# A four-layer graph network on one core: the last step of its layer normalisation on two other engines, the graph's self-loops selected later, and all jobs in a new order

## The chip, the core and the metric

The kernel runs on one core of a Trainium2 chip. A core has five engines that run their own instruction streams in order and meet through semaphores: TensorE (matrix products, into PSUM), VectorE, ScalarE, GpSimd (called POOL in the profile, without access to PSUM) and SyncE, which issues most DMAs here. The metric is the device time of one execution in microseconds (us); smaller is better. A measurement is given as the median of several runs.

## What is computed

Inputs are x, 32 batches of 512 nodes with 64 features, and one 512 x 512 adjacency matrix with weights. Four layers follow one another, each on a normalised and rectified copy of x and each with a residual addition. Everything is float32. Cut to what matters:

```python
def _layernorm(x, axis=-1, eps=1e-5):
    m = jnp.mean(x, axis=axis, keepdims=True)
    v = jnp.var(x, axis=axis, keepdims=True)
    return (x - m) / jnp.sqrt(v + eps)

h = jnp.maximum(_layernorm(x), 0.0); x = x + L0(h, adj)   # 3 steps: v = W2 relu(W1 [v, adj v] + b1) + b2; node 0 is replaced first
h = jnp.maximum(_layernorm(x), 0.0); x = x + L1(h, adj)   # 2 layers: z = relu((adj z) W)
h = jnp.maximum(_layernorm(x), 0.0); x = x + L2(h, adj)   # 8 attention heads and one output head, scores h hT masked by adj
h = jnp.maximum(_layernorm(x), 0.0); x = x + L3(h, adj)   # attention with leaky-ReLU scores, adj with ones on its diagonal
```

## The kernel before

**Pairs.** The 32 batches are worked in 16 pairs. Nodes lie on the 128 partitions, so one pair's x is a tile of 128 x 512 (four blocks of nodes, two batches, 64 features).

**Jobs.** The program is cut into named jobs. A job `p.name` belongs to pair p. Each issues a few instructions on one or more engines, and the order in which the jobs are called is the program order of every engine's stream. Three strings give that order: HEAD and TAIL list jobs of given pairs, and ROUND lists `name:lag`, which is repeated for every pair with the pair's number shifted by the lag. Jobs that HEAD or TAIL names are left out of the rounds. No engine passes an instruction that waits, so a job's place decides both what it waits behind and what waits behind it.

**Names that matter here.**
- `F0` to `F32` (function `front`): layers 0 and 1 of a pair, in 33 steps. F0 to F2 are the first normalisation: F0 the mean (VectorE) with centring and squares (GpSimd, L423 and L425); F1 the sum of squares (VectorE, L428) and the power -1/2 (GpSimd, L432); F2 the last step z (L435), then node 0's row (L541, VectorE) and b2 added to x (L542, GpSimd). F3 and F4 transpose z. F5 to F16 are the three steps of layer 0, F17 and F18 the residual x1, which also loads the x of the pair after next. F19 to F21 normalise x1, F22 to F29 are layer 1 (L485 is the aggregation over the graph), F30 to F32 normalise x2.
- `zT`, `zE`: features transposed; `k`, `Y`: keys of two heads (L1139, L1150).
- For a unit of two heads (letters a to d and g to j) or of the output attention (f) and the last layer (e): `s` scores on TensorE (L641, L644), `r` masked product with the row maximum on VectorE (L650), `m` the maximum negated on GpSimd (L663), `x` exponentials on ScalarE (L670), `nA`, `nB` reciprocal on VectorE and scaling on GpSimd (L682), `t` 32 x 32 transposes on VectorE (L688), `v` the weighted sums on TensorE (L697, L925, and L1022 for the last pair). Scores have four PSUM buffers, which `r` frees.
- `us`, `w`, `y`, `o`, `c`: eviction, the head's weights (L738), leaky ReLU (L750), output projection (L758), joining.
- `oA`, `oB`, `oC`: the normalisation ahead of the last layer; `oA0`, `oA1` and so on for the last pair, whose two batches go separately.
- `loops0` to `loops3` (L376): four selections each on GpSimd, which put ones on the diagonal of A3, the third copy of the graph in SBUF; only jobs `r…e` read A3. `factor0` to `factor3` (L371) prepare the second copy, A2, `masks` the mask; `graph0` to `graph3` transpose the first copy.
- `ZQ`, `hQ`, `lQ`, `LQ`, `OQ`: DMAs that spread values over partitions.

**Loads.** SyncE issues, in order, x of pair 0, the graph's first copy, small weights, x of pair 1, A2 in two halves and A3 in two halves.

Of the kernel before, what the change touches and what calls it, by code (L numbers as in the profile page):

```python
# [21 lines left out]
def gnn_stack_kernel(  # L22
# [40 lines left out]
        0.weights 0.F0 0.joined 0.F1 0.F2 0.F3 0.F4 0.biases 0.F5 0.F6 0.graph2 0.graph3 0.graph1 0.graph0 1.F0 0.F7  # L63
        0.F8 0.bjoined 0.F9 0.loops1 0.loops0 0.F10 0.F11 0.masks 0.loops3 0.F12 1.F1 0.factor1 0.F13 0.F14
        0.factor2 0.F15 0.F16 0.F17 1.F2 0.factor3 0.F18 0.grams 0.F19 0.F20 1.F3 2.F0 0.F21 0.F22 0.F23 0.F24 0.F25
        0.F26 1.F4 0.F27 1.F5 0.factor0 0.F28 0.F29 1.F6 0.F30 1.F7 0.F31 1.F8 0.vectors 0.F32 2.F1 0.zT 0.zE 0.k0
        0.Y0 1.F9 0.s0a 1.F10 0.s1a 0.r1a 0.ZQ11 0.r0a 0.r2a 0.m0a 0.x0a 0.s3a 0.r3a 0.s2a 0.m1a 0.r7a 0.r6a 0.r4a
        0.ZQ13 0.x1a 0.s1b 0.m3a 0.r5a 0.s0b 0.k1 0.x3a 0.m2a 0.x2a 0.nAa 0.r3b 0.r2b 0.r1b 0.r0b 0.m1b 0.Y1 0.s3b
        0.nBa 0.t0a 0.r6b 0.s2b 0.r4b 0.r7b 0.x1b 0.m0b 0.ZQ01 0.t1a 0.x0b 0.ZQ03 0.r5b 0.s0c 0.s1c 0.m2b 0.m3b
        0.t2a 1.F11 0.x2b 0.nAb 0.r1c 0.r2c 0.x3b 0.r0c 0.r3c 0.nBb 0.t3a 1.F12 0.t0b 0.m1c 0.t1b 0.m0c 0.x1c 0.s3c  # L70
        1.F13 0.ZQ02 1.F14 0.t3b 0.ZQ00 0.ZQ10 0.x0c 0.t2b 0.r7c 0.r6c 0.s2c 0.vA0 0.vB0 0.r4c 2.F2 0.r5c 0.m3c
        0.s0d 0.m2c 0.vC0 0.vD0 0.r1d 0.nAc 0.r0d 0.s1d 0.m0d 0.x3c 0.t0c 0.x2c 0.us0 0.s2d 0.t1c 0.w00 0.x0d 0.w10
        0.nBc 0.r3d 0.y00 0.r2d 0.t2c 0.m1d 0.t3c 0.ZQ12 0.r5d 0.s3d 0.r7d 0.k2 0.loops2 0.r6d 0.y10 0.o0 0.x1d
        0.r4d 0.m3d 0.Y2 0.x3d 0.m2d 0.nAd 0.c0 0.x2d 0.s1g 1.F15 1.F16 0.r2g 0.s0g 0.t0d 0.nBd 0.t1d 0.r3g 0.t2d
        1.F17 0.t3d 0.s3g 1.F18 0.r7g 0.vA1 0.r6g 0.vB1 1.F19 0.r0g 0.r1g 0.m1g 0.vC1 3.F0 1.F20 0.m3g 0.x1g 0.vD1
        0.m0g 0.s0h 0.s1h 0.r0h 0.r1h 0.us1 0.w01 0.s2g 0.x0g 0.r3h 0.r2h 0.x3g 0.s2h 0.y01 0.k3 0.nAg 0.m0h 0.r4g
        0.r5g 1.F21 0.r4h 0.r5h 0.Y3 0.m2g 0.t0g 0.x2g 0.s3h 0.w11 0.r6h 0.m2h 0.m1h 0.s2i 0.y11 0.nBg 0.x1h 0.x2h
        0.t1g 1.F22 0.r4i 0.s0i 0.t2g 1.F23 1.F24 0.r7h 0.m3h 0.r5i 0.x3h 0.x0h 3.F1 0.s1i 0.r0i 0.nBh 1.F25 0.r1i
        0.o1 0.r3i 0.t3g 0.r2i 0.nAh 1.F26 0.t2h 0.t3h 0.m0i 1.F27 0.t0h 0.t1h 0.s3i 1.F28 0.s1j 0.c1 1.F29 0.m1i
        1.F30 0.x1i 0.vA2 0.r6i 0.m2i 0.vB2 0.x2i 0.x0i 0.vC2 0.r7i 0.vD2 0.s2j 0.r2j 0.m3i 1.F31 0.x3i 0.nAi 0.r3j  # L80
        0.us2 1.F32 1.zT 0.m1j 2.F3 0.nBi 0.s0j 1.zE 0.r5j 0.r4j 2.F4 0.w12 0.t0i 0.x1j 2.F5 0.t2i 0.s3j 1.ZQ00 2.F6
        0.r1j 0.r7j 1.k0 0.y12 0.r0j 0.r6j 0.w02 0.m2j 0.m0j 1.Y0 0.x2j 1.s0a 1.s1a 2.F7 0.t1i 1.r1a 0.m3j 0.t3i
        0.x0j 0.x3j 0.y02 0.nAj 1.r3a 1.r0a 0.D0 1.r2a 2.F8 1.ZQ01 0.t0j 1.m1a 0.o2 1.k1 1.s3a 0.nBj 1.x1a 0.f0
        1.s2a 0.t1j 0.t2j 1.Y1 0.c2 1.m0a 0.t3j 0.vA3 0.vB3 1.ZQ02 1.r4a 1.x0a 1.r5a 1.nAa 0.vC3 0.vD3 1.m2a 1.r7a
        0.us3 1.t1a 1.x2a 3.F2 1.r6a 1.m3a 1.t0a 1.s1b 1.s0b 1.r2b 1.x3a 1.r3b 1.m1b 1.x1b 2.F9 1.ZQ10 1.r1b 1.ZQ12
        1.r0b 1.m0b 2.F10 1.x0b 1.s3b 1.ZQ11 1.s2b 1.nBa 1.r7b 1.r4b 1.r6b 1.m3b 0.w13 1.r5b 1.t2a 0.y13 0.w03 1.x3b
# [24 lines left out]
        t2c:0 r2d:0 oN:2 s0d:0 w00:0 r3d:0 oV:2 r1d:0 s2d:0 r0d:0 s3d:0 m1d:0 r4d:0 x1d:0 m0d:0 w10:0 r5d:0 y00:0
        x0d:0 r7d:0 m2d:0 oD:2 oF:2 r6d:0 s1f:1 m3d:0 x2d:0 x3d:0 nAd:0 F15:-1 de:2 r3f:1 t3c:0 t0d:0 nBd:0 r2f:1
        y10:0 k2:0 t1d:0 t2d:0 F16:-1 t3d:0 o0:0 Y2:0 s6e:2 ZQ10:0 F17:-1 hQ1:1 c0:0 F18:-1 s0e:2 vA1:0 r0e:2 F19:-1
        s3e:2 s7e:2 r7e:2 s1e:2 vB1:0 r3e:2 s2e:2 r6e:2 lQ2:2 s0f:1 r2e:2 m3e:2 r1e:2 m1e:2 s5e:2 m0e:2 s4e:2 x0e:2
        m1f:1 F20:-1 r0f:1 x1e:2 hQ2:1 r5e:2 r1f:1 x3e:2 vC1:0 r4e:2 m2e:2 s3f:1 x2e:2 F21:-1 s2f:1 x1f:1 nAe:2
        vD1:0 m0f:1 us1:0 r7f:1 r6f:1 r4f:1 t0e:2 nBe:2 s0g:0 r5f:1 t1e:2 r1g:0 hQ3:1 m3f:1 s1g:0 x0f:1 w01:0 r2g:0
        r0g:0 w11:0 m2f:1 x3f:1 y01:0 nAf:1 x2f:1 m0g:0 r3g:0 t3e:2 t0f:1 y11:0 s3g:0 t2e:2 nBf:1 lQ1:2 x0g:0 lQ0:2
        s2g:0 r7g:0 r6g:0 F22:-1 m1g:0 F23:-1 o1:0 r4g:0 r5g:0 lQ3:2 t1f:1 m3g:0 s1h:0 m2g:0 t2f:1 c1:0 F24:-1 t3f:1
        x1g:0 F25:-1 ZQ12:0 s0h:0 x3g:0 nAg:0 r0h:0 r3h:0 r2h:0 x2g:0 vAE:1 r1h:0 m0h:0 m1h:0 vBE:1 vCE:1 x1h:0
        x0h:0 vDE:1 nBg:0 F0:-3 eu:1 t1g:0 t2g:0 s2h:0 t0g:0 s3h:0 nAh:0 t3g:0 r5h:0 r4h:0 t0h:0 r6h:0 k3:0 Y3:0  # L120
        r7h:0 m2h:0 et:1 s1i:0 s0i:0 m3h:0 ZQ13:0 x2h:0 er:1 F26:-1 x3h:0 r3i:0 r0i:0 nBh:0 r1i:0 t1h:0 t2h:0 r2i:0
        F27:-1 s3i:0 F28:-1 s2i:0 t3h:0 F29:-1 m0i:0 vA2:0 vB2:0 x0i:0 vC2:0 m1i:0 x1i:0 F30:-1 r4i:0 r7i:0 r6i:0
        F2:-2 m3i:0 F31:-1 nAi:0 r5i:0 m2i:0 vD2:0 x3i:0 s2j:0 F32:-1 t0i:0 us2:0 zT:-1 s1j:0 zE:-1 F3:-2 r5j:0 oA:1
        w12:0 x2i:0 F4:-2 r3j:0 r4j:0 r2j:0 y12:0 m2j:0 s0j:0 m1j:0 x1j:0 s3j:0 t1i:0 k0:-1 nBi:0 w02:0 r6j:0 r0j:0
        Y0:-1 r1j:0 r7j:0 t3i:0 s1a:-1 m3j:0 F5:-2 s0a:-1 r2a:-1 t2i:0 y02:0 m0j:0 r0a:-1 F6:-2 x0j:0 nAj:0 x3j:0
# [1220 lines left out]
```

## Time and profile before

| | |
|---|---|
| median of 3 runs | 2108.91 us |
| the three runs | 2110.44, 2103.96, 2108.91 us |
| the profiled execution | 2107.21 us |
| its span (first to last instruction) | 2105.4 us |
| mean granted clock of TensorE | 0.986 |
| A3's copies issued / landed | 29.2 and 29.8 / 42.5 us |
| first scores (L641) | 86.8 us |
| first weighted sums (L697) | 109.8 us |
| a repeat of the round | 123.08 us |
| the last twentieth (1998.8 to 2105.4): TensorE busy | 77.2 of 106.6 us |

The profile is that of one execution. Its first part gives each engine's busy time. Its second cuts the span into 40 slices of 52.6 us, and a digit is the busy share of a slice in tenths. A group of instructions has its line, engine, operation, output and inputs with shapes and count, then busy time and mean nanoseconds of one, then the engine's idle time ahead of it with what ended that. The chain of waits is followed back from the last instruction: at each step to whatever released it, or to the instruction before it on its engine. "issue" is time in which the profile shows nothing that was waited for. The ends of matrix products are modelled, so a busy TensorE is not always at its peak.

### The profile page before, as it was taken

The numbers are of one execution on the slowest core, as the hardware profiler recorded it, in microseconds if no ns is written. First come the engines' busy times: TensorE is split into PE (matmuls) and PEld (weight loads), VectorE is DVE, ScalarE is ACT, GpSimd is POOL, SyncE is SP. The second block draws the span as 40 slices with busy tenths as digits, with TensorE's granted clock in tenths as the row PEclk, the third lists the DMA queues.
The fourth block names the chain that finished last, engine by engine and source line by source line (L and its number), as shares of the span: only waits on it lengthen the run. The fifth ranks groups of instructions, "written<-read, shape, count | busy, mean of one in ns | idle before, by whom it ended". The sixth has DMA issues, their size and how long they took to land.

```text
span 2105.4 us, 91065 instructions
## 1 busy us (share of the span) xinstructions
PE 2023.7 (96%) x38941; PEld 1218.5 (58%) x38941; DVE 1842.8 (88%) x4205; ACT 1468.8 (70%) x3796; POOL 1274.8 (61%) x2161
## 2 busy tenths in 40 slices
PE   5799999999999999999999999999999999999985
PEld 3356566565556656555665655666565565655554
DVE  3588888989999999999999999999999998899955
ACT  1366667778686777867677786767778677677845
POOL 2356565766666576666657666665766656566543
PEclk9899999999999999999999999999999999999997
DMA  6101101112121111212111111111111111111213
GB/s 135 25 9 27 28 20 34 31 27 43 28 42 26 34 30 27 41 30 42 26 33 27 31 38 33 38 30 32 27 33 38 31 36 35 41 26 33 41 32 74
DMA packets 257626, 74.46 MB, mean 35 GB/s; under 512 B 240324, under 2 KB 249668, under 8 KB 257220
## 3 DMA queue, kind: packets, MB, share of 16 engines
q1 hardware_dynamic: 256768, 68.54, 15.6%
q8 instruction: 305, 5.00, 1.0%
q14 instruction: 101, 0.83, 0.1%
q10 hardware_dynamic: 452, 0.10, 0.0%
HBM read 16.52 MB, written 4.78 MB: 10 GB/s over the span
## 4 chain that ended last, share of the span: by engine, by line
PE 79%; DVE 11%; ACT 3%; POOL 2%; issue 2%; DMA 2%; SPq 0%; ACTq 0%; DVEq 0%; POOLq 0%
PE s L641 21%; PE mm L697 18%; PE mm L758 5%; PE mm L925 5%; PE mm L508 5%; PE s L644 5%; PE mm L738 5%; PE mm L485 4%; DVE sm L688 4%; DVE sm L650 4%; PE mm L1139 3%; PE mm L511 3%; ACT sm L670 2%; POOL sm L682 1%; PE mm L533 1%
## 5 line engine op out<-in xcount | busy, mean ns | idle before, releaser
L670 ACT ACTIVATE sm<-sm,nmx 128x512 f32<-128x512 f32 x1280 | 909.3, 716 | 221.7 <-POOL nmx L663 217.6
L682 POOL TENSOR_SCALAR sm<-sm,rs 128x512 f32<-128x512 f32 x1280 | 873.6, 704 | 275.7 <-DVE rs L680 263.9
L650 DVE CUSTOM_DVE_ANT_0 sm<-s,A 128x512 f32<-128x512 f32 x1264 | 808.1, 678 | 43.5 <-PE s L644 41.2
L688 DVE STREAM_TRANSPOSE sm<-sm 128x1024 f32<-128x1024 f32 x640 | 776.4, 1229 | 78.7 <-POOL sm L682 77.0
L641 PE MATMUL s<-ZZ,Y 64*64 64x512 f32 x4096 | 568.8, 600 | 5.9 <-DVE mx L650 5.7
L697 PE MATMUL mm<-sm,vq 32*64 32x256 f32 (+1 forms) x16640 | 492.9, 376 | 3.9 <-DVE sm L688 3.1
L697 PEld LDWEIGHTS mm<-sm,vq 32*64 32x64 f32 x16640 | 399.3, 132 | 106.9 <-issue 53.8
L663 POOL TENSOR_SCALAR nmx<-mx 128x2 f32<-128x2 f32 x640 | 141.4, 233 | 304.3 <-DVE mx L650 236.3
L641 PEld LDWEIGHTS s<-ZZ,Y 64*64 64x64 f32 x4096 | 143.1, 133 | 185.2 <-DVE mx L650 67.4
L644 PE MATMUL s<-NEGM,I2b 64*64 64x512 bf16 x2288 | 249.3, 376 | 0.0
L670 ACT ACTIVATION_READ_ACCUMULATOR sm<-sm,nmx 128x1 f32 x1280 | 246.3, 192 | 0.0
L644 PEld LDWEIGHTS <-I2b 64*64 64x64 bf16 x2288 | 81.2, 107 | 151.2 <-issue 148.9
L750 ACT ACTIVATE y<-mm,cols 128x512 f32<-128x512 f32 x256 | 161.1, 686 | 9.1 <-PE mm L738 7.6
L738 PE MATMUL mm<-us,Wh 64*64 64x512 f32 x1024 | 141.5, 590 | 1.3 <-ACT hT L478 0.8
L432 POOL TENSOR_TENSOR r<-ve,mhalf 128x8 f32<-128x8 f32 (+1 forms) x65 | 106.3, 1636 | 59.6 <-DVE ve L430 50.8
L423 POOL TENSOR_TENSOR xc<-x,nmu 128x512 f32<-128x512 f32 (+1 forms) x49 | 50.3, 1026 | 142.2 <-DVE nmu L421 135.6
L732 ACT COPY us<-mm 128x256 f32<-128x256 f32 x256 | 76.1, 380 | 85.1 <-PE mm L697 85.1
L485 PE MATMUL mm<-AT,z 128*128 128x512 f32 x256 | 121.4, 618 | 7.1 <-DVE z L435 6.3
L758 PE MATMUL mm<-y,Wo_sb 128*64 128x256 f32 x1024 | 124.1, 384 | 2.1 <-ACT y L750 2.1
L508 PE MATMUL mm<-AT,v 128*64 128x256 f32 x1024 | 117.6, 382 | 0.1
L925 PE MATMUL mm<-sm,vq 32*64 32x256 f32 x3712 | 111.4, 376 | 0.6 <-issue 0.6
L925 PEld LDWEIGHTS mm<-sm,vq 32*64 32x64 f32 x3712 | 101.1, 132 | 13.7 <-DVE rs L680 7.1
(151 smaller groups left out, 1875.6 us busy)
## 6 DMA issues: line engine op xcount, KB each, us to landing
vq<-z SPq DMA_DIRECT2D x512, 32.0 KB
HH<-cat SPq DMA_DIRECT2D x128, 64.0 KB
vq<-catT SPq DMA_DIRECT2D x240, 32.0 KB
vq<-h3n SPq DMA_DIRECT2D x240, 32.0 KB
A<-in_adj_dram SPq DMA_DIRECT2D x5, 1024.0 KB
xt<-in_x_dram SPq DMA_DIRECT2D x32, 128.0 KB
ZZ<-ZZ SPq DMA_DIRECT2D x32, 128.0 KB
out_dram<-xo SPq DMA_DIRECT2D x32, 128.0 KB
```

The costliest lines, as they stand in the source:

```text
L485: nc.tensor.matmul(pe, lhsT=v[:, m].rearrange("p j d -> p (j d)"), rhs=AT[:, m, :], start=(m == 0), stop=(m == NT - 1),)
L508: nc.tensor.matmul(ph[out_, :], lhsT=v[:, m, j, :], rhs=AT[:, m, h], start=False, stop=stop)
L641: nc.tensor.matmul(pss[half][R[ab], :], lhsT=lhsT, rhs=rhs, start=True, stop=False)
L644: nc.tensor.matmul(pss[half][R[ab], :], lhsT=I2b[R[half], :], rhs=NEGM[R[half], k, :], start=False, stop=True)
L650: nc.vector.tensor_tensor_reduce(self.sm[:, s, :], self.pss.pop(s), self.graph(s), 1.0, -FMAX, ALU.mult, ALU.max, self.small("mx", slice(s ...
L670: nc.scalar.activation(self.sm[:, s, :], self.sm[:, s, :], AF.Exp, bias=self.small("nmx", slice(s, s + 1)), accum_out=self.small("ssum", s ...
L682: nc.gpsimd.tensor_scalar(self.sm[:, s, :], self.sm[:, s, :], self.small("rs", slice(s, s + 1)), 1.0, ALU.mult, ALU.mult)
L688: nc.vector.transpose(out=two, in_=two)
L697: nc.tensor.matmul(self.u[i][R[c], 0 : weights.shape[1] * 32], lhsT=values[32 * i : 32 * i + 32, jb, :], rhs=weights[32 * i : 32 * i + 32, ...
L738: nc.tensor.matmul(self.py[ab][c][r, :], lhsT=Wh2[R[c], self.head(c, ab), r], rhs=self.us[R[c], 2 * ab : 2 * ab + 2].rearrange("p i (s e) ...
L758: nc.tensor.matmul(self.pa[R[half], 0 : N // 2], lhsT=Wo_sb[:, self.head(k, ab), :], rhs=self.y[self.head(k, ab)][:, half * N // 2 : (half ...
L925: nc.tensor.matmul(self.u[i][r, 0 : N // 2], lhsT=values[q, jb, :], rhs=unit.sm[q, :, 32 * jb : 32 * jb + 32], start=(jb == 0), stop=(jb = ...
```

## The change

In `ln_relu`, z = max(xc, 0) * r was one VectorE instruction. It becomes a product on GpSimd and a Relu in place on ScalarE. It is used four times per pair: in F2, F21, F32 and oC.

```diff
@@ ln_relu
         z = bp.tile([P, NS, D], F32, tag="b", name="z")[:, :g]
-        nc.vector.scalar_tensor_tensor(
-            z, xc, 0.0, r.unsqueeze(2).to_broadcast([P, g, D]), ALU.max, ALU.mult
-        )
+        nc.gpsimd.tensor_tensor(z, xc, r.unsqueeze(2).to_broadcast([P, g, D]), ALU.mult)
+        nc.scalar.activation(z, z, AF.Relu)
         return z
```

HEAD, ROUND and TAIL are written anew with the same jobs. HEAD grows from 748 to 754 jobs, TAIL from 1263 to 1450, and ROUND keeps its 388. The start of HEAD, the places of the loops and of F2, F32 in ROUND:

```diff
@@ HEAD
-        0.weights 0.F0 0.joined 0.F1 0.F2 0.F3 0.F4 0.biases 0.F5 0.F6 0.graph2 0.graph3 0.graph1 0.graph0 1.F0 0.F7
-        0.F8 0.bjoined 0.F9 0.loops1 0.loops0 0.F10 0.F11 0.masks 0.loops3 0.F12 1.F1 0.factor1 0.F13 0.F14
-        0.factor2 0.F15 0.F16 0.F17 1.F2 0.factor3 0.F18 0.grams 0.F19 0.F20 1.F3 2.F0 0.F21 0.F22 0.F23 0.F24 0.F25
-        0.F26 1.F4 0.F27 1.F5 0.factor0 0.F28 0.F29 1.F6 0.F30 1.F7 0.F31 1.F8 0.vectors 0.F32 2.F1 0.zT 0.zE 0.k0
-        0.Y0 1.F9 0.s0a 1.F10 0.s1a 0.r1a 0.ZQ11 0.r0a 0.r2a 0.m0a 0.x0a 0.s3a 0.r3a 0.s2a 0.m1a 0.r7a 0.r6a 0.r4a
...
-        0.nBc 0.r3d 0.y00 0.r2d 0.t2c 0.m1d 0.t3c 0.ZQ12 0.r5d 0.s3d 0.r7d 0.k2 0.loops2 0.r6d 0.y10 0.o0 0.x1d
...
+        0.F0 0.F1 0.weights 0.biases 0.joined 0.bjoined 0.F2 0.F3 0.F4 0.graph0 0.graph3 0.graph1 1.F0 0.graph2 0.F5
+        0.F6 0.F7 0.F8 0.F9 0.F10 0.F11 1.F1 0.F12 0.F13 0.factor0 0.F14 0.F15 0.F16 0.F17 0.masks 0.F18 0.grams
+        0.F19 0.F20 0.F21 0.F22 1.F2 0.F23 0.F24 1.F3 0.factor3 2.F0 0.F25 0.F26 0.F27 0.F28 0.F29 0.F30 0.vectors
+        0.F31 0.F32 0.zT 0.zE 0.k0 1.F4 0.ZQ03 0.factor2 0.factor1 0.Y0 0.loops1 0.k1 0.s1a 0.s0a 0.ZQ13 0.r2a 0.r3a
+        0.m1a 0.Y1 0.x1a 1.F5 0.r1a 0.s2a 0.r0a 1.F6 0.ZQ12 0.ZQ01 0.r5a 0.r4a 0.m0a 0.s3a 0.m2a 0.r6a 0.s0b 0.r7a
+        0.m3a 0.x0a 0.nAa 0.r1b 0.r0b 0.s1b 0.r2b 0.x2a 0.r3b 0.m1b 0.m0b 0.x3a 0.x1b 0.x0b 0.ZQ00 0.k2 0.s3b 0.t0a
+        0.nBa 0.r6b 0.r7b 0.s2b 0.ZQ02 0.r5b 0.r4b 0.t2a 1.F7 0.m2b 0.m3b 0.x2b 0.nAb 0.s0c 1.F8 1.F9 0.x3b 0.t3a
...
+        0.vB1 0.r1g 0.vC1 0.s1g 0.s3g 0.r2g 0.vD1 1.F21 0.r6g 0.s1h 0.r3g 0.m0g 0.r7g 0.x0g 0.loops2 0.s0h 0.m1g
...
+        3.F1 1.r4d 1.x2c 1.s0d 1.vB0 1.vC0 1.vD0 1.r0d 1.x3c 1.r5d 1.r1d 0.hQ1 1.s3d 1.x1d 0.loops0 1.m0d 1.x0d
+        1.us0 1.t1c 0.hQ3 1.nBc 1.ZQ11 0.loops3 1.r7d 0.f1 0.s1f 1.r6d 1.m3d 1.w10 1.y10 1.w00 0.s2f 0.r3f 1.t3c
@@ ROUND
-        F27:-1 s3i:0 F28:-1 s2i:0 t3h:0 F29:-1 m0i:0 vA2:0 vB2:0 x0i:0 vC2:0 m1i:0 x1i:0 F30:-1 r4i:0 r7i:0 r6i:0
-        F2:-2 m3i:0 F31:-1 nAi:0 r5i:0 m2i:0 vD2:0 x3i:0 s2j:0 F32:-1 t0i:0 us2:0 zT:-1 s1j:0 zE:-1 F3:-2 r5j:0 oA:1
...
+        t2h:0 t3h:0 s2i:0 F29:-1 F2:-2 hQ1:0 vA2:0 F30:-1 r6i:0 r5i:0 x1i:0 vB2:0 m0i:0 r4i:0 r7i:0 m2i:0 F31:-1
+        vC2:0 x2i:0 x0i:0 F32:-1 m3i:0 vD2:0 nAi:0 s2j:0 us2:0 oA:1 zT:-1 r5j:0 r4j:0 s1j:0 zE:-1 F3:-2 ZQ03:-1
```

## The prediction

> **What bounds the kernel now.** I read the page's engine totals and its 40 slices first, to see where in the span TensorE is not full.
>
> ```profile
> PE 2023.7 (96%) x38941; PEld 1218.5 (58%) x38941; DVE 1842.8 (88%) x4205; ACT 1468.8 (70%) x3796; POOL 1274.8 (61%) x2161
> ...
> PE   5799999999999999999999999999999999999985
> DVE  3588888989999999999999999999999998899955
> ...
> PEclk9899999999999999999999999999999999999997
> ```
>
> TensorE is below nine tenths only in the first two and last two slices (52.6 us each). From some 160 to 1735 us it is full at the full granted clock, and VectorE is second at 88%. So an edit can win in three places: the head, the tail, and the few microseconds of each round in which a "busy" TensorE runs slower than it can. The second view is the chain of waits in the head.
>
> ```profile
> 29.84 12.60 DMA A<-in_adj_dram
> 42.48 0.07 issue
> 42.58 0.23 POOL A L376
> ...
> 45.34 0.24 POOL A L376
> 45.58 1.62 POOL r L432
> 47.23 1.76 DVE z L435
> 49.00 0.22 DVE z L541
> 49.22 1.13 DVE A L371
> 50.35 0.67 DVE x L579 x2
> ...
> 58.53 6.69 PE mm L485 x8
> ```
>
> Read it downward. GpSimd reaches twelve selections of the graph (L376, jobs loops1, loops0, loops3) and stands there until the last copy of the graph, A3, has landed at 42.5. The list of waits puts that at 16.5 us, once. Behind the selections in GpSimd's queue is the power (L432) of pair 1's normalisation; behind that, in VectorE's queue, z of pair 1; and behind that x1 of pair 0 (L579), whose products TensorE had ended at 39.4. TensorE is empty for 8.9 us, and for 6.3 us more while pair 0's second normalisation runs.
>
> The third view is one repeat of the round. The L485 block that starts at 1117.82 comes again at 1240.90, so a round is 123.08 us. The lines are that stretch's window row (span, then busy time of PE, PEld, DVE, ACT, POOL, then clock and DMA), two pieces of its chain, and one row of TensorE's timeline.
>
> ```profile
> 1117.82:1240.90 123.08, 122.75 (x2413) 73.23 (x2413) 114.16 (x262) 91.32 (x238) 79.64 (x134) 1.00 0.16 33
> ...
> 1149.25 0.98 DVE z L435
> 1150.25 1.18 DVE z L541
> ...
> 1159.17 0.65 PE L641 MATMUL s<-ZZ,Y 64*64 64x512 f32 x2 [0.33 <-DVE mx L650]
> ```
>
> From 1138 to 1161 the chain runs on ScalarE, VectorE and GpSimd, and TensorE pays at its end: from 1156.92 to 1163.23 it does 8 L738 (0.86 us by the chain's unhindered pieces), 16 L641 with 8 L644 (twice 0.86 + 0.22), 16 L1139 (0.86) and 8 L738 (0.86). That is 4.74 us of work in 6.31, so 1.6 us a round are lost to VectorE, and z with its patch row is 2.2 us of the VectorE chain that makes the loss.
>
> **Part 1: z as a product and a Relu.** 65 VectorE instructions go and 65 go to each of GpSimd and ScalarE. Durations, from the groups by shape:
>
> ```profile
> L435 DVE SCALAR_TENSOR_TENSOR z<-xc,r 128x512 f32<-128x512 f32 x63 | 51.7, 821 | 27.2 <-POOL r L432 27.2
> L423 POOL TENSOR_TENSOR xc<-x,nmu 128x512 f32<-128x512 f32 x47 | 49.0, 1043 | 142.2 <-DVE nmu L421 135.6 <-DMA vq<-z 6.7
> ```
>
> The product has the form of L423 (one tile, one broadcast column): 1.04 us. A Relu of 128x512 in place is not in the trace. From below it is bounded by the 128x512 copy out of PSUM (L1150, 0.59), from above by the 128x512 Prelu with a bias column that reads SBUF (L879, 0.69). I take 0.62: Relu and copy of 128x256 cost the same (L597 0.38, L732 0.38), and its operand is in SBUF as L879's is.
>
> Load: VectorE loses 51.7 us, GpSimd gains 63 x 1.04 = 66, ScalarE 63 x 0.62 = 39. In a round (four normalisations) VectorE goes from 114.2 to 110.9, GpSimd from 79.6 to 83.8, ScalarE from 91.3 to 93.8; none reaches TensorE's 122.8, which is what hides them. Latency: a normalisation gets 1.04 + 0.62 - 0.82 = 0.84 us longer. In the round that is hidden by TensorE's other jobs: in the new list z stands 6 to some 30 jobs ahead of its use, nearest from F32 to zT, with vD2 and s2j (1.8 and 1.1 us of TensorE) between. In the head it is on the path.
>
> New wait: in job F2 the row copy L541 (VectorE) now needs the Relu, so VectorE stands for up to 1.04 + 0.62 = 1.7 us once a round, with the next score maxima, which free TensorE's score buffers, behind it. In the new round F2 stands right behind t2h, t3h (VectorE, 1.23 each) and F29 (two additions of 0.40), in which GpSimd and ScalarE can do product and Relu, and right ahead of vA2 and vB2 (TensorE, 1.8 each), which need no score buffer. I cost it at 0; without that cover it costs 1.7 a round.
>
> Value in the round: z (0.98) leaves the chain that makes the loss of 1.6. Bounds: nothing to 0.98 by that row, or the whole 1.6. I take half of 0.98, 0.5 us, times the 13 rounds that are full: 6.5 us.
>
> The Trainium skill (GPSIMD Engine Reference, "Engine selection"; ScalarE: Activation LUTs, "Rules for kernel authors") speaks against this part: elementwise work belongs on VectorE, GpSimd being about twice as slow with two inputs, and Relu is named as work not to give to ScalarE. The trace agrees on the size (1.04 against VectorE's 0.69 median). By that rule the added 0.84 us is loss; it is the last rival below.
>
> **Part 2: the selections later.** In the new order loops1 follows 0.Y0, and loops2, loops0, loops3 come in later rounds, long after 42.5 us. Their 16 x 0.24 us of GpSimd stay. x1 of pair 0 no longer waits: 50.35 - 39.4 = 10.9 us off the head's path. What is late next is pair 0's own normalisation (mean, centring, square, sum, power, z: 8.1 us from 50.35 to 58.40), which stays and keeps TensorE empty.
>
> **Part 3: the head's order.** F1 now stands ahead of the weights' jobs, so the sum of squares (L428) no longer waits behind the two W1T copies until 11.86; the squares are there at 7.34. Power, product and Relu then end near 11.8, the bias jobs' VectorE work at some 12.8, and z's transposition (L473, 16.55 now) starts near 13.1. The four transpositions of the graph (3.7 us) and F5 follow, and F7 starts near 20.0 instead of 23.07: 3.0 us. Two of pair 0's three normalisations are already in these sums but for the change of z in place: the second's z was 1.53 and becomes 1.7 (+0.2), the third's 0.69 becomes 1.7 (+1.0). Pair 0's first scores, at 86.8 now, should start at 86.8 - 10.9 - 3.0 + 1.2 = 74.1.
>
> Given back: pair 1's F5 and F7 (0.46 + 0.43 + 3.6 = 4.5 us) run now in TensorE's gap at 71 to 77.5; the new order has F7 only after the first scores. But from 87 to 112 VectorE is the limit (23.5 us busy of 25 by the window row of that stretch), so most of it fits there: I give back 1.5, bounds 0 and 4.5. Head: 12.7 - 1.5 = 11 us, bounds 5 (all given back and the 3.0 not gained) and 13. From 112 us on TensorE is full, so an earlier start is an earlier end.
>
> **Part 4: the rest of the order.** Round and tail hold the same jobs. Counted in the lists, a round has 30 changes of TensorE's tile size before and 29 after, so no cost there. Twelve jobs change their lag, most because the list is cut at another place; the DMA jobs (hQ, ZQ, lQ) keep their number. The tail, 106.6 us from 1998.8 with TensorE busy for 77.2, is a chain through the last pair. Its two 128x256 normalisations get GpSimd's 0.62 (L423, 128x256) and 0.38 for VectorE's 0.42: about 1 us. I can price nothing else in it and take 0, bounds 5 each way.
>
> **Sum.** 2105.4 (span) - 11 - 6.5 + 1 = 2088.9. The profiled execution took 2107.2, 1.8 more than its span, and the median is 1.7 above it: 2092.4, so 2092. Its own range: 2080 to 2101.
>
> **Rivals.**
> - Head alone: the round stays at 123.1, since TensorE is busy 122.75 of it. 2092 + 6.5 = 2099. For it: the window row; against: the 1.6 us. 0.20.
> - The round loses all of the 1.6: 13 x 1.6 = 21 instead of 6.5, so 2078. For it: VectorE's relief of 3.3 is twice the loss; against: the chain there also holds Exp and transposes. 0.11.
> - The reordering gives the head back (a later wait, the tail's chain): within 6 us of 2109. 0.09. Within 0.3% (6.3 us) is what a measurement of this kernel can't tell from no change.
> - Slower: the wait of L541. If F2's cover is missing because GpSimd is still in a normalise job (2.7 us for four tiles, L682) ahead of the product, VectorE stands 1.7 us in each of 16 pairs, score buffers stay full and TensorE pays: +27, no gain in the round: 2109 - 11 + 1 + 27 = 2126. It decides once a stand costs TensorE more than 11/16 = 0.7 us a pair. For it: VectorE is 93% busy in the round, so nothing is caught up; against: the order described in part 1. 0.13.
> - Slower, every step exposed: 63 x 0.84 = 53, 2109 - 11 + 53 = 2151. Against it: features lie far ahead of their use. 0.04. This is what the skill's rule would make of it.
>
> **How the numbers follow.** Forecast 0.43, head alone 0.20, whole loss 0.11: faster 0.74. Same 0.09, slower 0.17. The range goes down to 2074 (head 13 and the whole 1.6 give 2076, and 2 for the tail) and up to 2118, which leaves out the two slower cases in most of their width.
>
> **What would show it.** Right: no wait of L376 on a DMA; first scores (L641) near 74; the L485 gap after x1 still some 6 us, with GpSimd's product 1.04 and a Relu near 0.62; a round of 122 to 123 us; VectorE near 1790 us busy. Wrong: a round of 124 or more, VectorE idle ahead of L541 on the Relu by over 0.7 us a pair, TensorE below nine tenths in the middle slices, or first scores later than 80.

## The result, and the profile after

| | before | after |
|---|---|---|
| median | 2109.06 us (2103.96 to 2110.44, 4 runs) | 2080.65 us (2079.38 to 2081.38, 4 runs) |
| ratio | 1 | 0.9869 (0.9852 to 0.9886) |
| span of the profiled execution | 2105.4 us | 2078.6 us |
| first scores | 86.82 us | 74.62 us |
| a repeat of the round | 123.1 us | 121.1 us |

The kernel became 1.3% faster. The forecast was 2092 us with a range of 2074 to 2118: the direction and the places of the gain held, and the gain is 28 us instead of 17. Line numbers of the changed kernel stand 14 higher up to the power (L432 is now L446) and 13 higher behind z; z itself is L449 (product, GpSimd) and L450 (Relu, ScalarE). In the kernels of the experiments the numbers shift by a few more; the operands name the instruction.

The page of the changed kernel, its engine totals, three rows of its slices, and the chain that ended last, by engine:

```profile
PE 2000.3 (96%) x38941; PEld 1205.1 (58%) x38941; DVE 1800.3 (87%) x4140; ACT 1498.7 (72%) x3861; POOL 1316.2 (63%) x2226
...
PE   6799999999999999999999999999999999999986
...
DVE  3688889999898999989899998989999879899964
...
PEclk9899999999999999999999999999999999999997
...
PE 89%; DVE 3%; ACT 2%; DMA 2%; SPq 2%; POOL 1%; issue 1%; ACTq 0%; DVEq 0%; POOLq 0%
```

TensorE's busy time fell by 23 us although it executes the same 38941 products: a "busy" TensorE that had waited between products waits less. The chain says the same from the other side. Before, 79% of it lay on TensorE and 11% on VectorE, now 89% and 3%. The same line of the kernel before:

```profile
PE 79%; DVE 11%; ACT 3%; POOL 2%; issue 2%; DMA 2%; SPq 0%; ACTq 0%; DVEq 0%; POOLq 0%
```

The groups by shape: total busy time, mean nanoseconds of one, then idle time ahead and its releaser.

```profile
L449 POOL TENSOR_TENSOR z<-xc,r 128x512 f32<-128x512 f32 x63 | 65.8, 1045 | 2.4
L450 ACT ACTIVATE z<-z 128x512 f32<-128x512 f32 x63 | 39.5, 627 | 66.7 <-POOL z L449 66.7
L554 DVE COPY z<-ivt 1x128 f32<-1x128 f32 x16 | 5.8, 363 | 4.5 <-ACT z L450 4.5
```

Product and Relu take 1.045 and 0.627 us. The Relus wait for their products for 66.7 us in all. In the rounds, where ScalarE has slack (93 of 121 us busy), TensorE never stands for one of them; it does three times outside, for 6.0 and 6.3 us in the head and 5.9 in the tail. VectorE's row copy, the place of the feared new wait, stands only once in the run, for 4.5 us in the head. Its own mean fell from 901 to 363 ns, of which more is said at the end.

One repeat of the round, as a window row (span, then busy PE, PEld, DVE, ACT, POOL, clock and DMA):

```profile
1100.00:1221.10 121.10, 120.75 (x2416) 72.39 (x2412) 111.83 (x258) 93.20 (x241) 81.80 (x137) 1.00 0.16 33
```

The round lost 2.0 us, and so did TensorE's busy time in it. VectorE went from 114.16 to 111.83. The chain of waits within this window runs on TensorE alone but for one piece of 0.57 us on ScalarE (an eviction of Y); before, VectorE had 7.1% of it in its transposes and masked products alone.

The head, some pieces of the chain of waits (start, duration, what):

```profile
32.35 10.87 DMA xt<-in_x_dram
43.31 2.04 POOL z L449 x2
45.37 0.64 ACT z L450
...
52.44 3.71 PE mm L498 x8
...
63.30 2.55 POOL r L446
65.93 1.05 POOL z L449
67.01 0.64 ACT z L450
67.69 1.15 PE mm L486 x32
...
75.18 0.28 PE s L654
```

GpSimd's stand on the last copy of the graph has left the chain; the selections now wait 0.5 us in all (17 before). What is left in its place is the normalisation that the prediction named: power, product, Relu, then TensorE. One DMA piece is still in the chain, the x of pair 2, which landed at 43.22. It can have cost next to nothing: GpSimd's power of pair 0's second normalisation (41.57, 1.65 us long) ends at the same moment, and the product that needs it starts at 43.30. Of the two products there ("x2"), the first is pair 0's, for which TensorE waits, and the second pair 1's.

Where the 26.8 us of span came from can be added up from the starts of one instruction, the last eviction of weighted sums of each pair (job us3). Differences after minus before:

| stretch | predicted | measured |
|---|---|---|
| start to pair 0's last eviction | -11 | -9.7 |
| the next 11 steps, pair to pair | -6.5 | -24.2 (123.2 to 121.1, and 2 to 3 us in each of the first two) |
| the two steps in which ROUND ends and TAIL begins | 0 | +6.9 (131.0 and 127.7 for 123.4 and 128.4) |
| the last two steps and the end | +1 | +0.2 |
| sum | -16.5 | -26.8 |

So the head was sized about right, the round was undersized by a factor of nearly four, and a loss at the passage from ROUND to TAIL was not foreseen.

### The profile page after: what moved, and what is told of

Its sections match the earlier page's. It is cut to its first block, busy times and chain, and to the rows that moved or that the text cites. A ratio compares the mean times of both kernels' runs of the same rounds, so it can differ in the third digit from the quotient of the medians.

```text
span 2078.6 us, 90978 instructions
## 1 busy us (share of the span) xinstructions
PE 2000.3 (96%) x38941; PEld 1205.1 (58%) x38941; DVE 1800.3 (87%) x4140; ACT 1498.7 (72%) x3861; POOL 1316.2 (63%) x2226
## 4 chain that ended last, share of the span: by engine, by line
PE 89%; DVE 3%; ACT 2%; DMA 2%; SPq 2%; POOL 1%; issue 1%; ACTq 0%; DVEq 0%; POOLq 0%
PE s L654 24%; PE mm L710 22%; PE s L657 6%; PE mm L498 5%; PE mm L771 5%; PE mm L938 5%; PE mm L751 5%; PE mm L521 5%; PE mm L1152 3%; PE mm L524 3%; PE mm L546 2%; DVE sm L701 1%; PE mm L486 1%; PE mm L1035 1%; DVE sm L663 1%; ACT sm L683 1%
## 5 line engine op out<-in xcount | busy, mean ns | idle before, releaser
L663 DVE CUSTOM_DVE_ANT_0 sm<-s,A 128x512 f32<-128x512 f32 x1264 | 803.4, 679 | 65.4 <-PE s L657 56.7
L654 PE MATMUL s<-ZZ,Y 64*64 64x512 f32 x4096 | 554.3, 598 | 6.3 <-DVE mx L663 4.8
L710 PE MATMUL mm<-sm,vq 32*64 32x256 f32 (+1 forms) x16640 | 485.5, 377 | 6.7 <-DVE sm L701 4.1
L710 PEld LDWEIGHTS mm<-sm,vq 32*64 32x64 f32 x16640 | 383.5, 132 | 122.3 <-issue 49.4
L676 POOL TENSOR_SCALAR nmx<-mx 128x2 f32<-128x2 f32 x640 | 131.0, 216 | 358.6 <-DVE mx L663 322.8
L657 PE MATMUL s<-NEGM,I2b 64*64 64x512 bf16 x2288 | 242.9, 376 | 0.0
L654 PEld LDWEIGHTS s<-ZZ,Y 64*64 64x64 f32 x4096 | 145.5, 133 | 164.2 <-issue 66.0
L657 PEld LDWEIGHTS <-I2b 64*64 64x64 bf16 x2288 | 80.3, 107 | 152.3 <-issue 150.7
L751 PE MATMUL mm<-us,Wh 64*64 64x512 f32 x1024 | 135.3, 593 | 0.0
L446 POOL TENSOR_TENSOR r<-ve,mhalf 128x8 f32<-128x8 f32 (+1 forms) x65 | 107.2, 1650 | 35.6 <-DVE ve L444 33.7
L938 PEld LDWEIGHTS mm<-sm,vq 32*64 32x64 f32 x3712 | 101.6, 132 | 14.9 <-PE s L657 7.9
L437 POOL TENSOR_TENSOR xc<-x,nmu 128x512 f32<-128x512 f32 (+1 forms) x49 | 50.3, 1027 | 93.9 <-DVE nmu L435 83.6
```

Of the source, the lines that this page charges most:

```text
L654: nc.tensor.matmul(pss[half][R[ab], :], lhsT=lhsT, rhs=rhs, start=True, stop=False)
L657: nc.tensor.matmul(pss[half][R[ab], :], lhsT=I2b[R[half], :], rhs=NEGM[R[half], k, :], start=False, stop=True)
L663: nc.vector.tensor_tensor_reduce(self.sm[:, s, :], self.pss.pop(s), self.graph(s), 1.0, -FMAX, ALU.mult, ALU.max, self.small("mx", slice(s ...
L710: nc.tensor.matmul(self.u[i][R[c], 0 : weights.shape[1] * 32], lhsT=values[32 * i : 32 * i + 32, jb, :], rhs=weights[32 * i : 32 * i + 32, ...
L751: nc.tensor.matmul(self.py[ab][c][r, :], lhsT=Wh2[R[c], self.head(c, ab), r], rhs=self.us[R[c], 2 * ab : 2 * ab + 2].rearrange("p i (s e) ...
L938: nc.tensor.matmul(self.u[i][r, 0 : N // 2], lhsT=values[q, jb, :], rhs=unit.sm[q, :, 32 * jb : 32 * jb + 32], start=(jb == 0), stop=(jb = ...
```

## The experiments

The kernel before took 2105.4 to 2106.3 us on the chips of these runs; ratios are to it. Three questions: which part of the change carries the round's 2.0 us, whether the selections carry the head, and what costs 7 us at the passage.

**z alone, in the old order.**

```diff
@@ ln_relu, before
-        nc.vector.scalar_tensor_tensor(z, xc, 0.0, r..., ALU.max, ALU.mult)
+        nc.gpsimd.tensor_tensor(z, xc, r..., ALU.mult)
+        nc.scalar.activation(z, z, AF.Relu)
```

> The kernel before with z as product on GpSimd and Relu on ScalarE, in the old order. If the round's gain (123.1 to 121.1 us) comes from VectorE's relief alone, the round falls to 121 to 122 and the time to 2085 to 2097, with the head as before (first scores near 87 to 89). If the new order is what makes the round, the round stays at 123 or grows, since the old order has z where VectorE did it at once: 2105 to 2125.

Measured: 2203.35 us, ratio 1.0457 (1.0434 to 1.048), 98 us slower, 65 of them in the same 11 steps. First scores at 90.94, a round of about 129.0. VectorE is busy for 1798.5 us, as little as in the changed kernel, so its load is not what counts. The round has one stand of TensorE. The timeline of this kernel around it, GpSimd, then ScalarE, then TensorE (start, duration, instruction, and in brackets idle time and releaser):

```profile
1201.95 1.05 POOL L435 TENSOR_TENSOR z<-xc,r 128x512 f32<-128x512 f32 x1
1202.95 1.27 POOL L541 TENSOR_TENSOR xt<-xt,b2bc 128x512 f32<-128x512 f32 x1
...
1205.18 1.66 POOL L432 TENSOR_TENSOR r<-ve,mhalf 128x8 f32<-128x8 f32 x1 [0.78 <-DVE rs L679]
1206.83 2.70 POOL L681 TENSOR_SCALAR sm<-sm,rs 128x512 f32<-128x512 f32 x4
...
1209.69 1.04 POOL L435 TENSOR_TENSOR z<-xc,r 128x512 f32<-128x512 f32 x1
...
1210.77 0.63 ACT L436 ACTIVATE z<-z 128x512 f32<-128x512 f32 x1 [4.81 <-POOL z L435]
1211.30 1.18 ACT L731 COPY us<-mm 128x256 f32<-128x256 f32 x4
...
1211.71 1.29 PE L472 MATMUL mm<-ident,z 64*64 64x64 f32 x30 [4.46 <-ACT us L731]
```

Read it from the bottom. TensorE stands 4.46 us for zT, by the profile on ScalarE's copy of `us`; that copy stands behind the Relu of F32; the Relu waits 4.81 us for its product; and the product, which is 1.04 us long, has come to GpSimd's head only at 1209.69, behind F2's product, the addition of b2, a power and a normalise job of 2.70 us. The power is F32's own: the product needs its r, which is there at 1206.84, and then stands behind the normalise job for 2.85 us. In the old list F32, `t0i`, `us2` and zT follow each other directly. The same instructions as in the changed kernel, 123 us apart: the order decides, and by this timeline it is the place in GpSimd's queue.

The stand costs more than its 4.46 us. The windows of the same kernel around it:

```profile
1207.00:1212.00 5.00, 0.54 (x15) 0.29 (x7) 2.60 (x5) 1.23 (x4) 4.78 (x7) 0.94 0.00 0
1212.00:1214.00 2.00, 2.00 (x40) 1.49 (x40) 0.00 (x0) 1.51 (x5) 1.04 (x1) 0.50 0.04 12
1214.00:1216.00 2.00, 2.00 (x48) 1.38 (x44) 0.89 (x3) 1.53 (x6) 0.00 (x0) 0.81 0.55 126
1216.00:1218.00 2.00, 2.00 (x24) 1.11 (x20) 2.00 (x5) 1.80 (x4) 0.43 (x2) 1.00 0.43 104
...
1337.65:1344.48 6.83, 4.58 (x80) 3.49 (x84) 2.39 (x8) 4.10 (x13) 3.36 (x5) 0.50 0.19 44
```

The granted clock (third number from the right) is 0.50 and 0.81 in the 4 us after it: 2 x 0.50 + 2 x 0.19 = 1.4 us more. In this round and one other the clock is low for 3.4 us, and these two took 127.8 and 127.9 us; in the other nine it is low for 6.8 us, as in the last line, and they took 128.8 to 129.5. Against the 123.1 of before that is 4.7 to 6.4 us a round, of the size of the stand and its clock (4.46 + 1.4 = 5.9 here). It is no exact account: the round shown is 4.8 us longer and not 5.9.

**The order alone, with z as one VectorE instruction.**

```diff
@@ ln_relu, after
-        nc.gpsimd.tensor_tensor(z, xc, r..., ALU.mult)
-        nc.scalar.activation(z, z, AF.Relu)
+        nc.vector.scalar_tensor_tensor(z, xc, 0.0, r..., ALU.max, ALU.mult)
```

> The changed kernel with z back on VectorE in one instruction: the new order alone. If VectorE's relief makes the round, the round goes back to 123 and the time to 2081 + 11 x 2.0 = 2103, with first scores still near 74. If the order makes it, the round stays at 121.1 and the time within 3 us of 2081.

Measured: 2102.41 us, ratio 0.9984 (0.9975 to 0.9993); first scores at 73.89. The same stretch of the round as a window row:

```profile
1100.00:1222.20 122.20, 121.74 (x2416) 73.08 (x2412) 113.16 (x262) 91.46 (x238) 78.09 (x134) 1.00 0.15 32
```

The new order takes 0.9 us from the round by itself and moving z another 1.1. The first scores come as early as with z moved, but by pair 0's last eviction 6.9 us of the head are left (9.7 with z moved). The 11 steps give 11.9, and the steps of the passage cost more than with z moved (133.3, 130.0 and 127.7 us; 131.0, 127.7 and 124.3 in the changed kernel; 123.4, 128.4 and 123.7 before), so little is left. Parts do not add up: +98 for z and -3 for the order make -28 together.

**The selections.** First in the old order, late; then in the new order, early again.

```diff
@@ HEAD, before
-        0.F8 0.bjoined 0.F9 0.loops1 0.loops0 0.F10 0.F11 0.masks 0.loops3 0.F12 ...
+        0.F8 0.bjoined 0.F9 0.F10 0.F11 0.masks 0.F12 ...
-        0.Y0 1.F9 ...
+        0.Y0 0.loops1 1.F9 ...
-        ... 0.loops2 0.r6d ...
+        ... 0.loops2 0.loops0 0.loops3 0.r6d ...
```

> The kernel before with the four selection jobs alone moved: loops1 behind 0.Y0, loops0 and loops3 behind loops2. If the wait on A3's copy is on the head's path, x1 of pair 0 comes 10 to 11 us earlier, first scores near 76 to 77, and the time is 2097 to 2100. If what is gained in the head is waited for again before the rounds start, first scores come earlier but the time stays at 2105 or more.

```diff
@@ HEAD, after
-        0.F6 0.F7 0.F8 0.F9 0.F10 0.F11 1.F1 ...
+        0.F6 0.F7 0.F8 0.F9 0.loops1 0.loops0 0.F10 0.F11 0.loops3 1.F1 ...
```

> The changed kernel with the selections back where they were (loops1 and loops0 behind 0.F9, loops3 behind 0.F11). GpSimd then ends them at 45.6, and pair 0's centring (L437, 38.41 in the changed kernel) starts there: 7.2 us later. Theory of the head: first scores near 82, time 2081 + 7 = 2088. If the head's start doesn't matter: 2081.

Measured: late in the old order, 2096.56 us, ratio 0.9958 (0.9943 to 0.9974), first scores at 75.05 and the round unchanged at 123.1. x1 of pair 0 starts at 39.41 instead of 50.35: 10.9 us earlier, which is the number of the prediction. Early in the new order, 2089.66 us, ratio 0.992 (0.9904 to 0.9937), 9 us above the changed kernel, first scores at 83.58. The chain of waits in its head:

```profile
30.04 11.68 DMA A<-in_adj_dram
41.85 0.23 POOL A L390
...
44.62 0.24 POOL A L390
44.86 1.61 POOL r L446
46.47 1.02 POOL xc L437
```

It is the stand of before again: the copy of the graph, the selections, then the power of another pair and pair 0's centring behind them in the same queue. The selections are worth 9 us in either order. Pair 0's last eviction says more: it starts at 200.6 us here, at 200.9 before and at 191.2 in the changed kernel. What the rest of the new order gains by the first scores (83.6 for 86.8) is given back by then, so nearly all of the head's 9.7 us is the selections'.

**Which of the four z's does the harm in the old order.** Four kernels on the first one, in each of which a part of z goes back to one VectorE instruction or to another engine.

```diff
@@ ln_relu, z alone
+        if one:      # F2 alone / F32 alone / F2 and F32, so that F21 and oC are left
+            nc.vector.scalar_tensor_tensor(z, xc, 0.0, r..., ALU.max, ALU.mult)
+        else:
             nc.gpsimd.tensor_tensor(z, xc, r..., ALU.mult)
             nc.scalar.activation(z, z, AF.Relu)
@@ ln_relu, z alone: the Relu on GpSimd too
-        nc.scalar.activation(z, z, AF.Relu)
+        nc.gpsimd.tensor_scalar(z, z, 0.0, None, ALU.max)
```

F2 back on VectorE:

> Old order, z on GpSimd and ScalarE except in F2, where it stays one VectorE instruction. In the run with z alone VectorE stood 49.5 us at node 0's row (L541) for the Relu, 15 times, and ScalarE stood 169.3 us at the Relu for the product, 51 times. If VectorE's stand in F2 makes the loss of 97 us (16 pairs x 3.3, and the score buffers behind it), it goes: 2105 to 2130. If ScalarE's queue makes it, three of four Relus are left: 2165 to 2190.

Product and Relu both on GpSimd:

> Old order, product and Relu both on GpSimd, so no instruction of ScalarE waits for a product, and VectorE still waits in F2. If ScalarE's stand makes the loss: 2105 to 2140, although GpSimd gets 63 x 0.7 = 44 us more. If VectorE's stand in F2 makes it: 2190 or more, and the wait of L541 stays at 50 us or grows.

F32 back on VectorE:

> Old order, z on GpSimd and ScalarE except in F32, where it stays one VectorE instruction. With z alone each round had one stand of TensorE of some 4.5 us, at the transposition of F32's features (L473, job zT), 50.7 us in the middle of the span. If F32 is the place (its product stands behind F2's product, the power and a normalise job in GpSimd's queue, and its Relu ahead of the eviction us2 in ScalarE's), the stand goes, the round is 123 to 125 and the time 2105 to 2130. If the longer step costs in all places alike, a quarter of the 97 us goes: 2175 to 2185, as when F2 was spared (2182.7).

Only F21 and oC moved:

> Old order, only the z of F21 and oC on GpSimd and ScalarE; F2 and F32 stay on VectorE. VectorE is relieved of 2 x 0.82 us a round. If the 1.0 us by which the round of the run before still lay over 123.1 is VectorE's stand at node 0's row, it goes and the round is 122.3 to 123.1: 2095 to 2107. If every z that moves costs in the old order, the round stays at 123.6 or more: 2112 to 2130.

| old order | us | ratio | round |
|---|---|---|---|
| all four moved | 2203.35 | 1.0457 (1.0434 to 1.048) | 129.0 |
| without F2 | 2182.72 | 1.0361 (1.0341 to 1.0381) | 128 |
| without F32 | 2140.53 | 1.0166 (1.0149 to 1.0183) | 124.1 |
| F21 and oC alone | 2123.91 | 1.0087 (1.0073 to 1.01) | 123.5 |
| all four, Relu on GpSimd | 2255.51 | 1.0708 (1.0689 to 1.0728) | 133.1 |

The theory that the loss is VectorE's stand in F2 falls: without it 21 us come back of 98, and the stand of TensorE is still there (3.9 us). The theory that it is ScalarE's queue, in which the Relu holds up `us`, is not borne out either: with the Relu off ScalarE the stand is longer, and its releaser is now z itself. (This kernel also gives GpSimd more work, so it does not price ScalarE's queue.) TensorE's timeline of that kernel:

```profile
1237.63 1.13 PE L472 MATMUL mm<-ident,z 64*64 64x64 f32 x32 [6.72 <-POOL z L436]
```

With F32 back on VectorE the stand is gone and the round is 124.1: F32's move was 4.9 of the 5.9 us, more than the 0.85 us by which its two instructions are longer than the one. Even F21 and oC alone lose 18 us. In the profiled execution, the fastest of that kernel, 13.1 us can be laid out: 0.5 in the head, 5.3 in the 11 steps, 1.5 at the passage and 5.8 behind it. So relief of VectorE gained nothing in any of these kernels of the old order.

In the list of waits of the kernel without F32, F2's stand is what the prediction's slower rival described:

```profile
DVE z L545 <- ACT z L441: 49.7, 15, 13.5
```

50 us in 15 stands (longest 13.5). In the changed kernel it is 4.5 us in one.

**The Relu on VectorE, in the new order.**

```diff
@@ ln_relu, after
-        nc.scalar.activation(z, z, AF.Relu)
+        nc.vector.tensor_scalar(z, z, 0.0, None, ALU.max)
```

> New order, product on GpSimd, Relu in place on VectorE. If load alone counts, VectorE takes 63 x 0.3 to 0.7 us, less than the 0.82 it lost: the round is 121.1 to 122.0 and the time 2081 to 2091. If a wait in VectorE's queue costs what its load doesn't (four stands a round for a product of 1.04 us), the round is over 122.2, that of the order with the single VectorE instruction: 2100 or more.

Measured: 2121.88 us, ratio 1.0078 (1.0054 to 1.0102), a round of 123.2. The Relu's group by shape:

```profile
L450 DVE TENSOR_SCALAR z<-z 128x512 f32<-128x512 f32 x63 | 30.5, 486 | 65.4 <-POOL z L449 65.4
```

It is shorter here (486 ns for 627), and VectorE as a whole has less to do than before the change (1814 for 1843 us). It waits 65.4 us for the products, as the Relu on ScalarE does (66.7); on ScalarE, with its slack, that is idle time, on VectorE what stands behind is late. 41 us lie between the two kernels, 23 of them in the 11 steps and 10 at the passage. That the wait makes them is argued from load and rows: it is what is left, since VectorE's load fell.

**The passage from ROUND to TAIL.** In the changed kernel TensorE stands there once for over 1.5 us. GpSimd and TensorE in its timeline:

```profile
1700.50 1.04 POOL L439 TENSOR_TENSOR sq<-xc 128x512 f32<-128x512 f32 x1 [5.51 <-DMA vq<-h3n]
...
1703.12 2.58 PE L654 MATMUL s<-ZZ,Y 64*64 64x512 f32 x8 [4.27 <-DVE mx L663]
```

and the granted clock in its windows after that:

```profile
1703.00:1705.00 2.00, 1.88 (x10) 0.75 (x14) 1.97 (x9) 0.00 (x0) 2.00 (x3) 0.60 0.00 0
1705.00:1707.00 2.00, 2.00 (x16) 0.90 (x12) 0.83 (x3) 1.55 (x4) 2.00 (x4) 0.55 0.03 8
1707.00:1709.00 2.00, 2.00 (x26) 0.90 (x22) 1.07 (x4) 1.65 (x4) 2.00 (x5) 1.00 0.00 0
```

GpSimd's squares wait 5.51 us for a transfer of h3n, VectorE's sum waits for the squares, and the score maxima stand behind that sum. With the clock, 4.27 + 2 x 0.40 + 2 x 0.45 = 6.0 us.

This stand lies in the second of the two steps (pair 12's eviction starts at 1649.8), which with 127.7 us is 0.7 shorter than before. The step that is longer than before is the first, 1518.8 to 1649.8, with 131.0 us for 123.4. It holds 60 products more than a round, 2472 for 2412: five times the 8 score products with 4 more (L654, L657) that the prediction priced at 0.86 + 0.22 us, so about 5.4 us by that price. The kernel before has three such groups more in its second step (2448). So a good part of the 131.0 is work that lies one step later before; over both steps the two kernels differ by 32 small products alone (4892 for 4860), and the 6.9 us of both is loss.

SyncE issues without a pause from 1656 to 1699, so the theory was that transfers of TAIL are queued there too densely. Three kernels on the changed one: the jobs of one more round left to ROUND; pair 11's lQ jobs gathered ahead; and these with the last pair's row loads (aO) far later as well.

```diff
@@ TAIL, jobs of one more round left to ROUND
-        12.r6g 11.nBf 12.r4g 10.lQ2 12.r5g 13.F23 ...
+        15.aO0 13.ZQ00 13.ZQ01 13.m1b 11.oC ...
@@ TAIL, lQ gathered
-        ... 11.lQ1 12.D1 ... 11.lQ0 12.r4f ... 11.lQ3 12.t1f ... 11.lQ2 14.F23 ...
+        ... 11.lQ1 11.lQ0 11.lQ3 11.lQ2 12.D1 ...
@@ TAIL, lQ gathered and rows late
-        ... 11.vCE 15.aO0 12.x0h ... 11.oV 15.aO2 13.r3d ... 15.aO3 13.k2 ... 15.aO1 13.x0c ...
+        ... 15.s1i 15.aO0 15.r5h ... 15.nAh 15.aO1 15.t2g ... 15.aO3 15.x0g 15.OS0 15.aO2 ...
```

> The changed kernel with TAIL's jobs of one more round left to ROUND, so that TAIL starts one round later; else the same. In the changed kernel the step from pair 11's to pair 12's last eviction is 131.0 us where a round is 121.1. If TAIL's own order there costs it (SyncE's backlog of DMA issues until 1699, for which GpSimd's squares wait 5.5 us), it becomes 121 to 123 and the time 2071 to 2075. If the passage from ROUND to TAIL costs it wherever it lies, the step moves one pair later: 2079 to 2084.

> The changed kernel with three spreading jobs in TAIL (11.lQ0, lQ3, lQ2) moved up to directly behind 11.lQ1, ahead of pair 12's. If SyncE's order of issues makes the stand of GpSimd's squares (5.5 us) and of TensorE (4.3 us) near 1700, both go and the time is 2075 to 2078. If the stand only finds another releaser: 2080 to 2082.

> As the run before, and the loads of the last pair's graph rows (15.aO0 to aO3), which in TAIL stand some three pairs ahead of their use and hold four tiles of the pool of 31, moved to just ahead of pair 15's last heads. If the pool is what is short in the passage to TAIL, 2070 to 2076; if not, the same as the run before within 1.5 us.

| on the changed kernel | us | ratio | steps at the passage |
|---|---|---|---|
| as it is | 2080.65 | 0.9869 (0.9852 to 0.9886) | 131.0, 127.7, 124.3 |
| one more round in ROUND | 2083.70 | 0.9894 (0.9875 to 0.9913) | 121.4, 140.1, 124.3 |
| lQ gathered | 2081.24 | 0.9888 (0.9873 to 0.9903) | 130.9, 129.5, 124.3 |
| lQ gathered, rows late | 2081.25 | 0.9886 (0.9871 to 0.9901) | 130.9, 125.2, 126.8 |

None of the three is faster, and each came out by the second branch of what was expected. With one more round the cost moves a pair later and does not shrink (385.8 us for the three steps, for 382.9). With lQ gathered this stand goes and another comes, TensorE's timeline there:

```profile
1686.37 1.64 PE L651 MATMUL s<-HH 64*64 64x512 f32 x3 [4.58 <-DMA HH<-cat]
```

The step of 131.0 stays at 130.9. With the rows late as well, the largest stand there is 2.46 us, and yet the three steps make 382.9 us, as in the changed kernel. So the stand accounts for about 6 us where it is, but it is not what sets the length of the passage. What does is open; none of the kernels tried was faster than the changed one.

## Why the prediction was right, and where its sizes were off

- **Reading of the places: right for head and round.** They were named as places where time could be won, and the round's "busy" TensorE as slower than it can be. TensorE's busy time fell by 23 us without a product less. The tail, priced at +1, measured +0.2.
- **The total: partly luck.** The round gave 17.7 us more than forecast and the passage took 6.9 back. Without that loss the time would have been about 2074, at the lower end of the range, so two errors of opposite sign brought the result nearer to the forecast.
- **Part 2, the selections: right.** 10.9 us of x1 was forecast and 10.9 measured when they alone were moved; 9 of them reach the end.
- **Part 3, the head: right within 1 to 2 us.** z's transposition started at 14.04 (13.1 forecast), F7 at 18.5 (20.0), the first scores at 74.62 (74.1). "I give back 1.5": by pair 0's last eviction 12.2 had become 9.7, so 2.5. With the selections early again nothing of this part was left there (200.6 for 200.9), so its 3.0 us were given back whole, within the bounds of 0 and 4.5.
- **Part 1, durations: right.** 1.04 and 0.62 were forecast for product and Relu, 1.045 and 0.627 measured; VectorE near 1790, measured 1800.3.
- **Part 1, "I cost it at 0" for L541's wait: right, by its cover.** One stand of 4.5 us in the run. The rival that made it slower is a real mechanism: in the old order the same wait is 50 us in 15 stands, and sparing F2 gave 21 us back. The cover it named, F2 behind t2h, t3h and F29 and ahead of vA2 and vB2, is what the new list has and the old one has not.
- **Part 1, "Value in the round ... I take half of 0.98, 0.5 us": the step that was off.** It measured 2.0 in a full round, of which, taken in this sequence, 0.9 are the order's and 1.1 are z's (1.1 against a bound of 0.98 by its row). What was missing is that the order also relieves VectorE: with z left there and the order new, the row copy L541 takes 215 ns instead of 901 and z 706 instead of 821, 0.69 + 4 x 0.115 = 1.15 us a round, of the size of the 0.9 (VectorE's busy time in the round falls from 114.16 to 113.16). That this relief is what gave the 0.9 was not tested by itself. And z's own part measured just above the bound that was set for it. The prediction had named "z with its patch row" as 2.2 us of the chain and then let only z's 0.98 leave it; the patch row went from 1.18 to 0.36 in the round as well. "The round loses all of the 1.6" (2078) was the nearest rival, and "head alone" (a round of 123.1) is out.
- **Part 4, "take 0": the other term that was off, both ways.** The new ROUND gave 0.9 a round, and the passage from ROUND to TAIL, which the prediction did not look at, took 7 back.
- **What the prediction took for one effect is a pair.** It priced z's move by load and latency, as a gain in itself. Alone it costs 98 us, most of it where F32's product queues on GpSimd. That the order has to fit stood in it only as cover for one wait (L541); the costlier place was F32, of which it said that two TensorE jobs lie between it and zT. In the old order there are one transpose and an eviction, and the round lost 4.9 us there. Which waits this order had to avoid was not in the sum, so that it avoided them is the order's merit and not the prediction's.
- **The rule that elementwise work and Relu belong on VectorE** (the Trainium skill, GPSIMD Engine Reference, "Engine selection", and ScalarE: Activation LUTs, "Rules for kernel authors"). The durations agree in direction: 1.045 + 0.627 against a mean of 0.821 for the single instruction. GpSimd's product alone takes 1.5 times VectorE's median of 0.69 for the whole step, so the prediction's "agrees on the size" is too strong for a rule that says about two. As a forecast the rule holds in the old order (4.6% slower) and not in the new one, where z back on VectorE is 22 us slower and the Relu alone back on it 41 us.

## What to carry to other kernels

Moving an operation off a loaded engine is priced at the place where it lands: ask what stands ahead of it in the new engine's queue and what stands behind it there, before counting its duration. An operation split over engines adds waits, and these belong on the engine with slack: with about 66 us of this wait on VectorE instead of ScalarE the kernel was 41 us slower. Where a change reorders everything, the seams between a repeated part and its ends are priced as well as the repeat.

## What the runs showed that was not expected

- **A stand of TensorE can cost more than its length, and the length alone does not decide it.** After stands of 4.3 to 4.6 us in the rounds and at the passage the granted clock fell to 0.50 for 3.4 or 6.8 us; that is 1.4 to 1.7 us more in the two cases worked out above. A stand of 2.17 us in the tail of the changed kernel left it at 1.00, but a stand of 2.17 us in the kernel with the order alone, of the same place, was followed by 0.50. The clock's records in the traces show a difference: in all 14 kernels the granted clock is 1.00 or 0.50, and it keeps each value for whole multiples of 3.41 us. On these steps the two stands read (first the order alone, then the changed kernel):

```profile
1869.14:1872.56 3.42, 1.25 (x11) 0.55 (x4) 2.85 (x4) 3.10 (x8) 2.20 (x4) 1.00 0.00 0
1872.56:1875.97 3.41, 3.41 (x6) 1.35 (x5) 2.28 (x2) 0.01 (x1) 1.28 (x3) 0.50 0.02 5
...
1846.74:1850.16 3.42, 2.35 (x86) 1.89 (x69) 2.02 (x2) 2.02 (x7) 2.71 (x4) 1.00 0.00 0
1850.16:1853.57 3.41, 2.31 (x6) 1.12 (x7) 1.71 (x4) 2.12 (x6) 2.88 (x5) 1.00 0.02 5
1853.57:1856.98 3.41, 3.19 (x56) 1.69 (x58) 2.68 (x4) 1.53 (x3) 0.00 (x0) 1.00 0.00 0
```

  In the first the whole stand lies in one step, in which TensorE is busy for 1.25 of 3.42 us, and the next step has 0.50. In the second it is split over two steps, 1.1 us in each, and the clock stays. Counted over the 14 traces, each of the 121 steps at full clock with more than 1.85 us of idle TensorE was followed by 0.50, and one of the 7983 with less than 0.85 was; of the 175 between, 40. So by these traces a short stand's price depends on where it falls on the steps; no run shifted one to test it. The Trainium skill (TensorE: Matmul & The Clock Gate, "Why this matters for your kernels") says to leave no gaps of more than about 3 us. The runs agree at 4.3 us, and show drops already behind stands of 2.2 us and, at 1932 us in the changed kernel, of 1.73.
- **What a VectorE instruction costs depends on what GpSimd does meanwhile.** The copy of one row of 1x128 took 901 ns on average in the old order, where it ran beside GpSimd's addition of b2; 363 in the changed kernel and 215 in the two others with the new order for which it was read (z, or its Relu, on VectorE). The group before and with the order alone, then a round's addition and copy in the kernel before and in the changed one:

```profile
L541 DVE COPY z<-ivt 1x128 f32<-1x128 f32 x16 | 14.4, 901 | 0.6
L555 DVE COPY z<-ivt 1x128 f32<-1x128 f32 x16 | 3.4, 215 | 0.6
...
1149.63 1.72 POOL L542 TENSOR_TENSOR xt<-xt,b2bc 128x512 f32<-128x512 f32 x1
1150.25 1.18 DVE L541 COPY z<-ivt 1x128 f32<-1x128 f32 x1
...
1119.89 1.28 POOL L555 TENSOR_TENSOR xt<-xt,b2bc 128x512 f32<-128x512 f32 x1
1120.89 0.36 DVE L554 COPY z<-ivt 1x128 f32<-1x128 f32 x1
```

  In both the copy ends 0.08 us behind the addition that had started before it (1151.43 and 1151.35, 1121.25 and 1121.17), however late it starts; with the order alone no addition was running when it started, and it took 215 or 216 ns each time. That the overlap is the cause was read from the timelines and not tested by itself.
